# A normalised, quantised convolution on one core: another order of work for images 126 to 145, another beginning, and the last image's result in two places of PSUM

## The chip, the cores and the metric

The kernel runs on one core of a Trainium2 chip. The metric is the device time of one execution in microseconds (us). The engines are called as in the profile: PE (TensorE, the matrix engine; PEld is its loading of weights), DVE (VectorE), ACT (ScalarE), POOL (GpSimd), and SP, which here only issues DMAs. PSUM is the memory that PE writes its results to; all else is held in SBUF.

## The reference

`x` is 160 images of 128 channels of 32 x 32, in fp32. There are five sets of weights, and each belongs to 32 images. Cut to what matters:

```python
beta, alpha = max(U), min(U)                 # over all five sets
s1 = (beta - alpha) / 3.0
v1 = s1 * floor(U / s1)
s2 = s1 / 5.0
v2 = s2 * floor((U - v1) / s2)
w = v1 + v2                                  # 3x3, 128 -> 128 channels, per set
# group norm of each image, 32 groups of 4 channels, eps 1e-5
act = conv(gn(x), w, stride 1, padding 1)    # image of set n by the weights of set n
out = x + act
```

So no weight is known before all five sets (590 KB each) have been read for their extremes.

## The kernel before, in words

**Weights at the beginning.** `run` (L782) issues the loads of the five weight sets on SP's queue; sets 0 and 1 come in two transfers each (L793 to L795), and the first image's load lies behind set 2 (L797 to L799). DVE reduces each piece to its maximum and minimum (`weight_range`, L422; L429 and L430). `over_partitions` (L437) brings the extremes to all partitions, over two transposes on PE; between these and the rest it calls a function that it is given, here PE's part of the means of the first two images (L827). DVE then does a chain of small steps (`from_range`, L50): s1, its reciprocal and parts, s2 and its own. A column of the 3 x 3 weights of set 0 is quantised in steps of 384 elements per partition on DVE (`quantise`, L116, `floor_div`, L104), turned by PE (L472, into PSUM tile pt) and kept by ACT and POOL (`keep_column`, L478, into tile wt). The columns come in the order 1, 0, 2 (`COLS`). `run` is an order written out by hand: `take` and `run` place single steps of the chain and the columns between the steps of the images, and every engine works in the order in which its instructions are written. `warm_up` (L644) is a row of matmuls whose result is not used.

**Images.** There are two kinds. For a *plain* image, ACT normalises it (z, L523) and rounds it to half precision (hi, L531); DVE takes the rest (lo, L589) and combinations of lo's rows (rows, L603 to L606). For a *combined* image, POOL and DVE make combinations of rows of x itself (L554, L555; `combine`, L565 to L571), ACT scales and rounds these (vh, L576) and DVE takes the rest (vl, L582). From image 7 on every second image is combined, from image 146 on two of three (`combined`, L534).

**One pass.** From image 3 on, pass i of the loop at L902 has PE compute first the sums and differences of row pairs of image i+1 (`sums_of_pairs`, L681, into two PSUM tiles called m, `self.pair`; the second one, a = 1, first), then the rest of image i (`rest_of_column`, L708, into its PSUM tile eo). PE takes few instructions for a combined image and more for a plain one. Beside that

- DVE does vl (or lo and rows) of image i+2, now and then the residual of image i-1, `pairs` of image i+1, and `combine` of image i+4;
- ACT does the first statistics pass (L194), the half of the result of image i-1 (sum, L754), the copy of one of m's tiles (L725), vh (or z and hi) of image i+3, and the second statistics pass (L201);
- POOL does outer rows, small steps of the statistics, and issues the DMA that adds sum to x (L773).

`pairs(i)` (L728) is two DVE instructions, L735 and L737, which add and subtract the two halves of m into a fresh eo tile, on which PE then accumulates the rest. eo tiles come from a pool of two (L376), the m tiles from a pool of one.

**Residual and store.** `residual(i)` (L746) is done by ACT and POOL, or "by hand" on DVE (L765): for images 31 on with i % 8 == 7, and for the last four, which are stored one by one from L769. The last image is computed in halves of 16 rows (L699), its residual and stores too (L757). All other stores are issued in `store` (L775) for two images at once.

**Weights later on.** The next sets are quantised on DVE in single steps between the images (`later`, L940; `take(later, ...)` at L967, L1005 and L1009). While the first images of a set are worked on, these steps lie between the two instructions of `pairs` and elsewhere.

Of the kernel before, what the change touches and what calls it, by code (L numbers as in the profile page):

```python
# [33 lines left out]
class Steps:  # L34
# [15 lines left out]
    def from_range(self, extg):  # L50


        nc, col = self.nc, self.col

        def divide_exact(tag, q1, a, m):

            q0, rem = col(tag + "q0"), col(tag + "rem")
            yield nc.vector.tensor_scalar_mul(q0, a, 1.0 / m)
            yield nc.vector.scalar_tensor_tensor(rem, q0, -(m - 1.0), a, ALU.mult, ALU.add)
            yield nc.vector.tensor_sub(rem, rem, q0)  # L60
            yield nc.vector.scalar_tensor_tensor(q1, rem, 1.0 / m, q0, ALU.mult, ALU.add)

        def parts(out, s):

            r, neg, hi, lo = out
            yield nc.vector.tensor_scalar_mul(neg, s, -1.0)
            yield nc.vector.reciprocal(r, s)
            yield nc.vector.tensor_single_scalar(
                hi.bitcast(I32), neg.bitcast(I32), -4096, op=ALU.bitwise_and
            )  # L70
            yield nc.vector.tensor_sub(lo, neg, hi)

        span = col("span")
        yield nc.vector.tensor_reduce(span, extg, AX.X, ALU.add)
        yield from divide_exact("s1", self.s1, span, 3.0)

        of_s1, s2 = parts(self.parts1, self.s1), divide_exact("s2", self.s2, self.s1, 5.0)
        for chain in (s2, of_s1, of_s1, s2, of_s1, s2, s2, of_s1):
            yield next(chain)
        yield nc.vector.tensor_scalar_mul(self.lift, self.s2, LIFT)  # L80
        yield from parts(self.parts2, self.s2)
        self.span, self.big = span, col("big")
        yield nc.vector.tensor_reduce(self.big, extg, AX.X, ALU.max)
# [228 lines left out]
class Main:  # L312
# [25 lines left out]
    LOAD_LEAD = 18  # L338
    STEADY = 7
    BY_VECTOR = (8, 10, 11, 14, 19, 24, 29, 34)  # L340
    THIRDS = 146
    EARLY = 8
    FIRST = 3
# [78 lines left out]
    def weight_range(self, us):  # L422

        nc, P = self.nc, self.P
        halved = [part for u in us[:2] for part in (u[:, : P // 2], u[:, P // 2 :])]
        pieces = [*halved, *us[2:]]
        ext = self.const.tile([P, 2, len(pieces)], F32, tag="ext", name="ext")
        for k, piece in enumerate(pieces):
            nc.vector.tensor_reduce(ext[:, 0, k : k + 1], piece, AX.XY, ALU.max)  # L429
            nc.vector.tensor_reduce(  # L430
                ext[:, 1, k : k + 1], piece, AX.XY, ALU.min, negate=True
            )
        ext1 = self.const.tile([P, 2], F32, tag="ext1", name="ext1")
        nc.vector.tensor_reduce(ext1, ext, AX.X, ALU.max)
        return ext1

    def over_partitions(self, ext1, ident, between):  # L437


        nc, P = self.nc, self.P  # L440
        rows = self.ps_tr.tile([1, 2, P], F32, tag="pt", name="rows")
        for k in range(2):
            nc.tensor.transpose(rows[:, k, :], ext1[:, k : k + 1], ident)
        between()
        top = self.const.tile([1, 2], F32, tag="top", name="top")
        nc.vector.tensor_reduce(top, rows, AX.X, ALU.max)
        spread = self.ps_tr.tile([P, 2], F32, tag="pt", name="spread")
        nc.tensor.matmul(spread, self.ones, top, start=True, stop=True)
        return spread
# [44 lines left out]
    def by_vector(self, i):  # L494
        return i in self.BY_VECTOR

    def stats_of(self, k):
        if k not in self.stats:
            self.stats[k] = Statistics(
                self.nc, self.small, self.ps_stat, self.gavg, self.mhalf, len(self.groups[k]),  # L500
                self.steps.lift, k,
            )
        return self.stats[k]

    def measure(self, i, stages=(0, 1)):


        k = self.group_of[i]
        g = self.groups[k]
        st, j, image = self.stats_of(k), i - g.start, self.image(i)  # L510
        if self.by_vector(i):
            st.image(j, image)
            return
        for s in stages:
            junk = self.unread.tile([self.P, 1024], MM, tag="junk", name=f"junk{i}_{s}")
            (st.image_sum, st.image_square)[s](j, image, junk)

    def normalise(self, i):
# [7 lines left out]
        )  # L526
        self.z[i] = z

    def high_part(self, i):
        hi = self.parts.tile([self.P, self.H, self.W], MM, tag="hi", name=f"hi{i}")  # L530
        self.nc.scalar.copy(hi.rearrange("p h w -> p (h w)"), self.z[i])  # L531
        self.hi[i] = hi

    def combined(self, i):  # L534

        if i < self.STEADY or i >= self.imgs:
            return False

        return i % 2 == 1 if i < self.THIRDS else i % 3 != 1

    def column_of(self, i):

# [96 lines left out]
        return self.ps_eo.tile([self.P, 2, self.H // 2, self.W], F32, tag="eo", name=f"eo{i}")  # L639

    def bank(self, target, h):
        return target[h] if target is self.pair else target[:, h]

    def warm_up(self, count):  # L644

# [47 lines left out]
    def conv(self, i, on_the_way):  # L693


        if self.FIRST < i < self.imgs - 1:
            self.sums_of_pairs(i + 1)

        for halves in ((0,), (1,)) if i == self.imgs - 1 else ((0, 1),):  # L699
            for col in self.COLS:  # L700
                if col == self.COLS[2] and i == self.FIRST:
                    self.sums_of_pairs(i + 1)
                if col != self.COLS[0] and halves[-1] == 1:
                    on_the_way(col)
                self.rest_of_column(i, col, halves)
        del self.v[i]

    def rest_of_column(self, i, col, halves):  # L708
        eo, both = self.eo[i], self.both(i)
        if not self.combined(i):  # L710
            self.taps(i, (self.hi[i], 0), col, eo, False, halves)
        for a, kind in enumerate((0, self.MINUS_G2)):
            for j, (d, _) in enumerate(both):
                for h in halves:
                    rows = slice(h * 16 + a, h * 16 + 16, 2)
                    to = eo[:, h].rearrange("p (i a) w -> p a i w", a=2)[:, a]
                    self.product(
                        to, i, kind, d[:, rows, :], col, False,
                        col == self.COLS[-1] and a == 1 and j == len(both) - 1,
                    )  # L720
# [7 lines left out]
    def pairs(self, i, between=lambda: None):  # L728


        nc = self.nc
        m1, m2 = self.pair[0], self.m2.pop(i)
        eo = self.eo[i] = self.bank_pair(i)
        rows = eo.rearrange("p h (i a) w -> p (h i) a w", a=2)
        nc.vector.tensor_add(rows[:, :, 0], m1, m2)  # L735
        between()
        nc.vector.tensor_sub(rows[:, :, 1], m1, m2)  # L737
# [44 lines left out]
    def run(self):  # L782
# [4 lines left out]
        for n in range(N_SETS):  # L787
            if n == 0:
                un = self.upool.tile([P, P, TAPS], F32, tag="u", name="u0")
            else:  # L790
                un = self.space(f"range{n}").rearrange("p j e -> p (j e)")[:, : P * TAPS]
                un = un.rearrange("p (i k) -> p i k", k=TAPS)
            half = P // 2 if n < 2 else P  # L793
            for c in range(0, P, half):
                nc.sync.dma_start(un[:, c : c + half], self.uv[n][:, c : c + half])  # L795
            self.us[n] = un
            if n == 2:  # L797
                self.chunks[0] = self.space("xt0")
                nc.sync.dma_start(self.chunks[0][:, 0, :], self.xv[0, :, 0, :])  # L799
        nc.sync.dma_start(self.chunks[0][:, 1, :], self.xv[0, :, 1, :])  # L800
        for c in range(1, 6):
            self.load(c, single=c < 2)
        warm = self.const.tile([P, 1], F32, tag="warm", name="warm")
        nc.vector.memset(warm, 0.0)
# [16 lines left out]

        self.ones = self.const.tile([1, P], F32, tag="ones", name="ones")
        nc.vector.memset(self.ones, 1.0)
        ext1 = self.weight_range(list(self.us.values()))
        for i in range(2):
            self.measure(i)
        spread = self.over_partitions(ext1, ident, self.stats_of(0).means)  # L827

        def take(steps, count):
            for _ in range(count):  # L830
# [13 lines left out]
        first, second, third = (  # L844
            self.make_column(0, col, by_scalar=col != self.COLS[0]) for col in self.COLS
        )
        for ahead in (11, 2, 1, 1, 1, 1, 1, 1):
            take(chain, ahead)
            take(first, 1)
        run(chain)  # L850
        self.stats[0].deviations()
        measure(0, 2, 3)
        self.stats[0].variances()
        self.stats[0].deviation()
        measure(1, 2)
        self.stats[0].scales()
        take(second, 1)
        measure(1, 3)
        self.stats[1].means()
        self.stats[1].deviations()  # L860
        self.warm_up(14)
        parts(0)
        self.stats[1].variances()
        self.warm_up(8)
        self.stats[1].deviation()
        self.stats[1].scales()
        parts(1)
        run(first)
        self.warm_up(2)
        parts(2)  # L870
        take(second, 2)
        self.low_part(0)
# [29 lines left out]
        for i in range(self.imgs):  # L902
# [58 lines left out]
            else:  # L961
# [3 lines left out]
                elif i + 2 < self.imgs:  # L965
                    self.low_part(i + 2)
                    take(later, 1)  # L967
                    run(self.combinations(i + 2))
                if i > self.FIRST and self.by_hand(j):
                    self.residual(j)  # L970
                for k in by_scalar:
                    self.measure(k, (0,))
# [10 lines left out]
                for st in ready:  # L983
                    st.deviations()
                if part:
                    self.normalise(i + 3)
                    self.high_part(i + 3)
                if self.combined(i + 3):
                    self.high_combined(i + 3)
# [12 lines left out]
            if i >= self.FIRST:  # L1002
# [3 lines left out]
                if self.combined(i + 4):  # L1006
                    self.combine(i + 4)
                else:
                    take(later, 1)  # L1009
                if b == self.per_set - 4:  # L1010
                    run(later)
# [61 lines left out]
```

## Time and profile before

| | |
|---|---|
| median of 5 runs | 991.95 us |
| lowest, highest | 991.81, 992.79 us |
| profiled execution | 992.12 us |
| its span, from first to last instruction | 990.40 us |
| mean granted PE clock | 0.998 |
| mean DMA rate | 248 GB/s |
| read from, written to HBM | 89.19, 83.89 MB |

The profiled execution is longer than its span by 1.72 us. Some of the costliest groups (columns: line, engine, operation, output and inputs with their shapes, count; then busy us in all and mean ns of one):

```
L582 DVE SCALAR_TENSOR_TENSOR vl<-v,rstd,vh 128x2048 f16<-128x2048 f32 x80 | 188.2, 2352 | 4.1 <-ACT vh L576 4.1
L576 ACT ACTIVATE vh<-v,rstd 128x2048 f16<-128x2048 f32 x80 | 160.8, 2010 | 2.5 <-POOL v L555 2.0
L523 ACT ACTIVATE z<-xt,shift,rstd 128x1024 f32<-128x1024 f32 x80 | 99.8, 1248 | 2.6 <-POOL shift L244 2.6
L589 DVE TENSOR_TENSOR lo<-z,hi 128x1024 f16<-128x1024 f32 x80 | 97.9, 1224 | 0.0
```

How to read it: the last part of a line is the idle time of the engine just ahead of such instructions, and what ended most of it. The mean of a group hides no idle time, but an instruction may start later than the one before it ended; durations "from start to start" count that gap. In a row of windows, each engine's busy time in the stretch is followed by its number of instructions. In a row of single instructions, the first number is the start in us from the span's start, the second the busy time, and what stands in brackets is the idle time ahead of it and its releaser.

### The profile page before, as it was taken

To read this page: it belongs to the slowest core of one execution; us is meant where nothing else is said; L and a number is where in the kernel's file an instruction comes from. 1 tells how busy PE (TensorE), PEld (TensorE's weight loads), DVE (VectorE), ACT (ScalarE), POOL (GpSimd) and SP (SyncE) were. 2 spreads that over 40 slices of the span, in tenths; PEclk is the share of its full clock that TensorE was granted. 3 is DMA by queue.
4 is the path that set the end of the run, shared out by engine and by line. 5 is a ranking of instruction groups with operands and counts; after the bars stand their busy time and mean duration, and the time that the engine had idled before them with its cause. 6 is when DMAs were issued, how large, how long until landed. Compare 5 with 4: busy or idle time off the path is not lost.

```text
span 990.4 us, 16124 instructions
## 1 busy us (share of the span) xinstructions
PE 959.7 (97%) x5938; PEld 578.8 (58%) x5938; DVE 928.5 (94%) x1256; ACT 895.6 (90%) x1224; POOL 387.5 (39%) x565
## 2 busy tenths in 40 slices
PE   2999999999999999999999999999999999999997
PEld 1445655566656666666665666666665666666564
DVE  7999999999999999999999999999999998889995
ACT  5879999999999999999999999999999999998651
POOL 4425563644316253414263443315343424132410
PEclk9999999999999999999999999999999999999999
DMA  9538999999997999898989999997999898987764
GB/s 357 211 103 238 237 255 274 257 265 270 260 303 181 298 249 294 237 282 244 273 218 266 274 279 236 281 282 223 237 280 304 214 300 217 293 227 206 180 178 153
DMA packets 65129, 246.05 MB, mean 248 GB/s; under 512 B 5008, under 2 KB 5008, under 8 KB 65040
## 3 DMA queue, kind: packets, MB, share of 16 engines
q1 hardware_dynamic: 45312, 173.09, 49.9%
q0 software_dynamic: 19728, 71.84, 37.7%
q8 instruction: 48, 0.79, 0.3%
q14 instruction: 41, 0.34, 0.1%
HBM read 89.19 MB, written 83.89 MB: 175 GB/s over the span
## 4 chain that ended last, share of the span: by engine, by line
PE 74%; DVE 12%; ACT 7%; issue 3%; POOL 2%; DMA 0%; SPq 0%; DVEq 0%; ACTq 0%; POOLq 0%
PE eo L668 24%; PE m L668 24%; PE eo L629 24%; ACT vh L576 2%; ACT junk L201 2%; ACT sum L754 1%; DVE eo L737 1%; DVE eo L735 1%; DVE lo L589 1%; DVE v L565 1%; POOL v L554 1%; DVE vl L582 1%; ACT m L725 1%; DVE v L568 1%; DVE v L571 1%
## 5 line engine op out<-in xcount | busy, mean ns | idle before, releaser
L668 PEld LDWEIGHTS <-wt 128*128 128x128 f16 x4266 | 417.2, 98 | 235.3 <-issue 7.2
L629 PE MATMUL eo<-hi,wt 128*128 128x496 f16 (+3 forms) x1422 | 340.8, 376 | 1.4 <-ACT wt L485 0.9
L773 POOL DMA_DIRECT2D xt<-sum x137 | 122.9, 903 | 460.2 <-ACT sum L754 445.5
L629 PEld LDWEIGHTS <-wt 128*128 128x128 f16 x1494 | 146.5, 99 | 142.5 <-issue 2.2
L582 DVE SCALAR_TENSOR_TENSOR vl<-v,rstd,vh 128x2048 f16<-128x2048 f32 x80 | 188.2, 2352 | 4.1 <-ACT vh L576 4.1
L668 PE MATMUL m<-vh,wt 128*128 128x496 f16 (+1 forms) x480 | 182.2, 380 | 2.0 <-DVE eo L737 1.2
L668 PE MATMUL eo<-vh,wt 128*128 128x248 f16 (+1 forms) x960 | 184.0, 273 | 0.0
L668 PE MATMUL eo<-vl,wt 128*128 128x248 f16 (+1 forms) x960 | 183.9, 273 | 0.0
L668 PE MATMUL m<-vl,wt 128*128 128x496 f16 (+1 forms) x480 | 182.2, 380 | 0.2 <-DVE vl L582 0.2
L194 ACT ACTIVATE junk<-xt 128x1024 f16<-128x1024 f32 x152 | 160.6, 1057 | 15.8 <-DMA xt<-in_x_dram 12.3
L201 ACT ACTIVATE junk<-xt,mv 128x1024 f16<-128x1024 f32 x152 | 173.8, 1144 | 0.1
L576 ACT ACTIVATE vh<-v,rstd 128x2048 f16<-128x2048 f32 x80 | 160.8, 2010 | 2.5 <-POOL v L555 2.0
L754 ACT ACTIVATE sum<-eo 128x1024 f32<-128x1024 f32 x137 | 138.2, 1008 | 15.3 <-PE eo L668 15.2
L735 DVE TENSOR_TENSOR eo<-m,m 128x512 f32<-128x512 f32 x157 | 109.1, 695 | 35.3 <-ACT m L725 28.2
L668 PE MATMUL eo<-rows,wt 128*128 128x256 f16 (+1 forms) x924 | 138.9, 273 | 0.0
L668 PE MATMUL m<-rows,wt 128*128 128x496 f16 (+1 forms) x462 | 113.6, 380 | 0.4
L737 DVE TENSOR_TENSOR eo<-m,m 128x512 f32<-128x512 f32 x157 | 109.4, 697 | 3.6
L725 ACT COPY m<-m 128x512 f32<-128x512 f32 x157 | 90.7, 577 | 18.4 <-PE m L668 18.4
L523 ACT ACTIVATE z<-xt,shift,rstd 128x1024 f32<-128x1024 f32 x80 | 99.8, 1248 | 2.6 <-POOL shift L244 2.6
L589 DVE TENSOR_TENSOR lo<-z,hi 128x1024 f16<-128x1024 f32 x80 | 97.9, 1224 | 0.0
L565 DVE TENSOR_TENSOR v<-xt 128x960 f32<-128x960 f32 x80 | 91.9, 1148 | 0.0
L531 ACT CAST hi<-z 128x1024 f16<-128x1024 f32 x80 | 83.6, 1045 | 2.5
(111 smaller groups left out, 892.4 us busy)
## 6 DMA issues: line engine op xcount, KB each, us to landing
xt<-in_x_dram SPq DMA_DIRECT2D x78, 1024.0 KB, 9.5
out_dram<-xt SPq DMA_DIRECT2D x78, 1024.0 KB, 5.9
xt<-sum POOLq DMA_DIRECT2D x137, 512.0 KB, 6.1
u<-in_L_conv_U_dram SPq DMA_DIRECT2D x4, 576.0 KB, 9.5
xt<-in_x_dram SPq DMA_DIRECT2D x4, 512.0 KB, 9.6
range<-in_L_conv_U_dram SPq DMA_DIRECT2D x3, 576.0 KB, 8.0
out_dram<-xt SPq DMA_DIRECT2D x3, 512.0 KB, 2.9
u<-in_L_conv_U_dram SPq DMA_DIRECT2D x2, 288.0 KB, 3.0
```

The lines of the kernel that those rows point to most:

```text
L194: self.nc.scalar.activation(junk, image, ACTF.Copy, scale=-1.0 / image.shape[1], accum_out=self.mv[:, j, 0:1],)
L201: self.nc.scalar.activation(junk, image, ACTF.Square, bias=self.mv[:, j, 0:1], accum_out=self.mv[:, j, 1:2],)
L565: nc.vector.tensor_sub(v[:, W:last], x[:, : last - W], x[:, 2 * W :])
L576: self.nc.scalar.mul(vh, self.v[i], st.rstd[:, j])
L582: self.nc.vector.scalar_tensor_tensor(vl, self.v[i], st.rstd[:, j], self.hi[i], ALU.mult, ALU.subtract)
L589: self.nc.vector.tensor_sub(lo[:, 1 : self.H + 1, :].rearrange("p h w -> p (h w)"), self.z.pop(i), self.hi[i].rearrange("p h w -> p (h w)"),)
L629: nc.tensor.matmul(self.bank(target, h)[:, r0 - h0 : r1 - h0, c0:c1], self.wts[n, col][:, k, :], tile[:, s0 : s0 + r1 - r0, c0 + dw : c1 + ...
L668: self.nc.tensor.matmul(target[:, :, c0:c1], self.wts[n, col][:, kind, :], source[:, :, c0 + dw : c1 + dw], start=start, stop=stop, skip_g ...
L735: nc.vector.tensor_add(rows[:, :, 0], m1, m2)
L737: nc.vector.tensor_sub(rows[:, :, 1], m1, m2)
L754: nc.scalar.mul(self.sum[i], eo.rearrange("p h r w -> p (h r w)"), 0.5)
L773: self.nc.gpsimd.dma_start(self.image(i), self.sum.pop(i), accum_op=ALU.add)
```

## The change

It has three parts.

1. **Images 126 to 145.** Combined are now the first, third and fifth of each five images (126, 128, 130, 131, 133, 135, ...), 12 of the 20 where it was 10. The fourth of each five (129, 134, 139; not 144, the first image of its statistics group) is plain, but its z is computed on DVE, by one tensor-scalar instruction at the end of pass i-4, where `combine` lies for combined images. ACT still makes its hi.
2. **The beginning.** Weight set 1 comes in one transfer. The first image's loads lie behind all five sets. The chain of small steps is s1, all parts of s1, s2, and so on, with no interleaving, and the steps of the first column are taken at other places of it. The statistics of images 0 and 1 are written behind the chain; PE's part of their means is no longer between the transposes and the rest. `warm_up` is called with 14 and 7 and no longer with 14, 8 and 2; the order of the parts of image 1 changes around it.
3. **The last image.** Its eo is two PSUM tiles, one per half of 16 rows, each with its own `pairs`. Those of the second half are made between PE's work on the two halves, behind the residual of image 158, since the eo pool still has two tiles.

The diff's core:

```diff
-        of_s1, s2 = parts(self.parts1, self.s1), divide_exact("s2", self.s2, self.s1, 5.0)
-        for chain in (s2, of_s1, of_s1, s2, of_s1, s2, s2, of_s1):
-            yield next(chain)
+        yield from parts(self.parts1, self.s1)
+        yield from divide_exact("s2", self.s2, self.s1, 5.0)
...
+    FIFTHS = 126
     THIRDS = 146
...
-        halved = [part for u in us[:2] for part in (u[:, : P // 2], u[:, P // 2 :])]
-        pieces = [*halved, *us[2:]]
+        pieces = [us[0][:, : P // 2], us[0][:, P // 2 :], *us[1:]]
...
+    def normalise_by_vector(self, i):
+        st, j = self.column_of(i)
+        z = self.z[i] = self.zpool.tile([self.P, 1024], F32, tag="z", name=f"z{i}")
+        self.nc.vector.tensor_scalar(
+            z, self.image(i), st.rstd[:, j], st.shift[:, j], ALU.mult, ALU.add
+        )
...
-        return i % 2 == 1 if i < self.THIRDS else i % 3 != 1
+        if i < self.FIFTHS:
+            return i % 2 == 1
+        return (i - self.FIFTHS) % 5 % 2 == 0 if i < self.THIRDS else i % 3 != 1
+
+    def by_vector_too(self, i):
+
+        if not self.FIFTHS <= i < self.THIRDS or (i - self.FIFTHS) % 5 != 3:
+            return False
+
+        return i != self.groups[self.group_of[i]].start
...
         for halves in ((0,), (1,)) if i == self.imgs - 1 else ((0, 1),):
+            if halves == (1,):
+                self.residual(i - 1)
+                self.pairs(i)
...
-        m1, m2 = self.pair[0], self.m2.pop(i)
-        eo = self.eo[i] = self.bank_pair(i)
-        rows = eo.rearrange("p h (i a) w -> p (h i) a w", a=2)
+        m1, m2 = self.pair[0], self.m2[i]
+        if i == self.imgs - 1:
+
+            h = len(self.eo.setdefault(i, []))
+            eo = self.bank_pair(f"{i}_{h}")[:, 0]
+            self.eo[i].append(eo)
+            part = slice(h * self.H // 4, (h + 1) * self.H // 4)
+            m1, m2 = m1[:, part], m2[:, part]
+        else:
+            eo = self.eo[i] = self.bank_pair(i)
+            eo = eo.rearrange("p h r w -> p (h r) w")
+        rows = eo.rearrange("p (i a) w -> p i a w", a=2)
...
-            half = P // 2 if n < 2 else P
+            half = P // 2 if n == 0 else P
...
-            if n == 2:
-                self.chunks[0] = self.space("xt0")
-                nc.sync.dma_start(self.chunks[0][:, 0, :], self.xv[0, :, 0, :])
-        nc.sync.dma_start(self.chunks[0][:, 1, :], self.xv[0, :, 1, :])
-        for c in range(1, 6):
+        for c in range(6):
             self.load(c, single=c < 2)
...
-        ext1 = self.weight_range(list(self.us.values()))
-        for i in range(2):
-            self.measure(i)
-        spread = self.over_partitions(ext1, ident, self.stats_of(0).means)
+        spread = self.over_partitions(self.weight_range(list(self.us.values())), ident)
...
-        for ahead in (11, 2, 1, 1, 1, 1, 1, 1):
+        for ahead in (8, 1, 1, 1, 1, 1, 3, 1, 1, 1):
             take(chain, ahead)
             take(first, 1)
         run(chain)
+        measure(0, 0, 1)
+        measure(1, 0, 1)
+        self.stats[0].means()
         self.stats[0].deviations()
         measure(0, 2, 3)
         self.stats[0].variances()
         self.stats[0].deviation()
+        take(second, 1)
         measure(1, 2)
         self.stats[0].scales()
-        take(second, 1)
         measure(1, 3)
         self.stats[1].means()
         self.stats[1].deviations()
         self.warm_up(14)
         parts(0)
         self.stats[1].variances()
-        self.warm_up(8)
         self.stats[1].deviation()
         self.stats[1].scales()
-        parts(1)
+        self.normalise(1)
         run(first)
-        self.warm_up(2)
+        self.warm_up(7)
+        self.high_part(1)
...
-                    self.normalise(i + 3)
+                    if not self.by_vector_too(i + 3):
+                        self.normalise(i + 3)
                     self.high_part(i + 3)
...
                 if self.combined(i + 4):
                     self.combine(i + 4)
                 else:
+                    if self.by_vector_too(i + 4):
+                        self.normalise_by_vector(i + 4)
                     take(later, 1)
```

More of the change, by code (lines that the diff above doesn't have):

```diff
@@ L435, in weight_range, with over_partitions @@
         return ext1
-    def over_partitions(self, ext1, ident, between):
+    def over_partitions(self, ext1, ident):
         nc, P = self.nc, self.P
@@ L443, in over_partitions @@
             nc.tensor.transpose(rows[:, k, :], ext1[:, k : k + 1], ident)
-        between()
         top = self.const.tile([1, 2], F32, tag="top", name="top")
@@ L495, in by_vector @@
         return i in self.BY_VECTOR
[L497 to L503, printed above, removed]
     def measure(self, i, stages=(0, 1)):
@@ L509, in measure @@
         g = self.groups[k]
-        st, j, image = self.stats_of(k), i - g.start, self.image(i)
+        if k not in self.stats:
+            self.stats[k] = Statistics(
+                self.nc, self.small, self.ps_stat, self.gavg, self.mhalf, len(g),
+                self.steps.lift, k,
+            )
+        st, j, image = self.stats[k], i - g.start, self.image(i)
         if self.by_vector(i):
@@ L527, in normalise @@
         self.z[i] = z
+    def normalise_by_vector(self, i):
[3 more added lines that the diff above has]
+            z, self.image(i), st.rstd[:, j], st.shift[:, j], ALU.mult, ALU.add
+        )
     def high_part(self, i):
@@ L641, in bank @@
     def bank(self, target, h):
-        return target[h] if target is self.pair else target[:, h]
+        return target[h] if isinstance(target, list) else target[:, h]
     def warm_up(self, count):
@@ L715, in rest_of_column @@
                     rows = slice(h * 16 + a, h * 16 + 16, 2)
-                    to = eo[:, h].rearrange("p (i a) w -> p a i w", a=2)[:, a]
+                    to = self.bank(eo, h).rearrange("p (i a) w -> p a i w", a=2)[:, a]
                     self.product(
@@ L968, in run @@
                     run(self.combinations(i + 2))
-                if i > self.FIRST and self.by_hand(j):
+                if i > self.FIRST and self.by_hand(j) and j in self.eo:
                     self.residual(j)
```

## The prediction

> **What bounds it.** I read the page's busy shares and clock row, then the windows of single stretches, the waits, and the order in time at three places.
>
> ```profile
> PE 959.7 (97%) x5938; PEld 578.8 (58%) x5938; DVE 928.5 (94%) x1256; ACT 895.6 (90%) x1224; POOL 387.5 (39%) x565
> ...
> PE 74%; DVE 12%; ACT 7%; issue 3%; POOL 2%; DMA 0%; SPq 0%; DVEq 0%; ACTq 0%; POOLq 0%
> ```
>
> PE bounds nearly everything, but DVE and ACT have 3 to 7% to spare, so what relieves PE must be weighed against both. Windows (columns: stretch, its us, PE, PEld, DVE, ACT, POOL busy, granted clock, DMA share, GB/s), of one plain and one combined image, and of two combined and one plain:
>
> ```profile
> 798.35:809.99 11.64, 11.64 (x74) 7.05 (x72) 10.06 (x14) 11.54 (x16) 1.45 (x3) 1.00 0.93 267
> ...
> 928.07:944.93 16.86, 16.86 (x111) 10.57 (x109) 16.61 (x19) 9.68 (x10) 3.93 (x8) 1.00 0.77 202
> ```
>
> PE is gapless in both. 16.86 − 11.64 = **5.22 us for a combined image**, 11.64 − 5.22 = **6.42 us for a plain one**: 1.20 us apart. From the order in time, a combined image is 2.59 (m) + 2.63 (eo), a plain one 1.30 + 5.12.
>
> **Part 1: images 126 to 145.** Combined images go from 10 to 12 of 20: PE −2 × 1.20 = **−2.40 us**. ACT: a combined image costs 1.90 from start to start (L576), a plain one 1.28 + 0.95 (L523, L531); common work is 3.70. Three combined, two plain, one z given away: 3 × 5.60 + 2 × 5.93 − 1.28 = 27.4 of PE's 3 × 5.22 + 2 × 6.42 = 28.5 in five images. DVE from start to start: combine 2.33, vl 2.26, lo with its rows 2.53, pairs 1.34, a by-hand residual 1.35. Five images: 3 × 5.93 + 2 × 3.87 + z 0.75 + 5/8 × 1.35 = 27.1 of 28.5. So it fits on average; the order decides.
>
> Pass i gives PE m(i+1), then eo(i): 7.71 if i is plain and i+1 combined, 3.93 the other way, 5.22 for two combined. DVE gets vl or lo of i+2, perhaps a residual, pairs(i+1), then combine or z of i+4. PE's second half of m(i+1) overwrites what pairs(i) reads, so a late pairs stops PE. The trace has one such place, just past three combined images:
>
> ```profile
> 917.42 0.70 DVE L735 TENSOR_TENSOR eo<-m,m 128x512 f32<-128x512 f32 x1
> ...
> 918.15 0.70 DVE L737 TENSOR_TENSOR eo<-m,m 128x512 f32<-128x512 f32 x1
> ...
> 918.42 0.38 PE L668 MATMUL m<-vl,wt 128*128 128x496 f16 x1
> ...
> 918.90 0.38 PE L668 MATMUL m<-vh,wt 128*128 128x512 f16 x1
> ```
>
> PE could have gone on at 918.64; it goes on at 918.90, as the second pairs instruction ends (918.85). I carried these durations through the new order by hand, each start being the latest of its engine's and its inputs' times. Done for the old order from 773.46 on, the end of the last matmul comes out at 983.93; the trace has 983.79. In the new order four places stop PE:
> - Pass 124. DVE used to end pass 122 at 773.77; combine(126) is now there: 773.24 + 2.33 = 775.57, vl(125) to 777.83, pairs(124) with a weight step in between to 779.79. PE would start that half at 778.83: **1.0 us**.
> - Pass 129. The residual of 127 used to lie in a pass of 7.71; pass 128 now has 3.93. DVE runs without a gap from pairs(127) at 794.77 (released by ACT's copy): 1.34 + 2.33 + 2.53 + 1.34 + 2.33 + 2.26 + 1.35 + 1.34 + 0.09 = 14.9, to 809.7. PE from 795.59: 2.59 + 5.12 + 1.30 + 2.63 + 1.30 = 12.9, to 808.5: **1.2 us**.
> - Passes 132 and 134: **0.4 and 0.5 us**, the same kind, after two combined images in a row.
> The other by-hand residual in a short pass (136) comes out without a gap, as DVE is less behind there. The stops sum to 3.1; the bookkeeping is 0.2 too hard on the old order, so I take 2.9: −2.4 + 2.9 = **+0.5 us**. Ends: all stops covered, −2.4; z at one element a cycle (no row has it: lo<-z,hi of the same size takes 1.22), +1.1.
> Z in between: nn<-rest, a tensor-scalar of 384 elements, takes 0.41, tt<-tt,s2r,nn, with two tensors, 0.61; the 0.2 less is 384 at half a cycle of about 1.04 ns, so I put z at 0.41 + 640 × 0.52 ns = 0.75. The Trainium skill's VectorE: DVE Perf Modes, Mode 2×_2P, says that a single-source fp32 instruction in SBUF gets two elements a cycle; at one a cycle the sum would be 0.4 higher.
>
> POOL's outer rows move with the combined images and have 60% free. No DMA is added; SP's stores move with PE.
>
> **Part 2: the beginning goes back.** The second weight set comes in one transfer, x0 behind all sets.
>
> ```profile
> 6.65 0.75 DVE L429 TENSOR_REDUCE ext<-range 128x1 f32<-128x576 f32 x1 [0.34 <-DMA range<-in_L_conv_U_dram]
> ...
> 9.30 1.34 DVE L429 TENSOR_REDUCE ext<-range 128x1 f32<-128x1152 f32 x1
> ...
> 39.06 0.46 PE L472 MATMUL pt<-ident,k 128*128 128x128 f16 x5 [1.38 <-DVE k L114]
> ...
> 40.10 2.69 PE L629 MATMUL eo<-hi,wt 128*128 128x496 f16 x6 [0.58 <-ACT wt L485]
> ```
>
> Two whole-set reductions take 2.52, four halves took 2.65, so DVE is even if set 1 lands at 6.78. The second half landed 5.1 after its issue at 2.14, at 7.24; with one issue less I take 7.1: DVE **+0.32**. In the chain of small steps s1r comes sooner and three small steps more lie among the big ones: 28.19 becomes 28.09, **−0.10**. Images 0 and 1 land at about 12.9 and 14.2 (10.1 and 14.3), so ACT and POOL run later: z(0) at 25.8 (23.59), hi(1) done at 32.15 (29.37), hi(2) at 34.4. DVE's lo(1) waits 0.2 more. Weight column 0 is ready 0.4 late and PE starts it at 40.6 (40.10). What hides that is PE's own pause, with the clock behind it:
>
> ```profile
> 38.00:39.00 1.00, 0.00 (x0) 0.00 (x0) 0.90 (x3) 0.00 (x0) 0.00 (x0) 1.00 0.00 0
> 39.00:40.00 1.00, 0.46 (x5) 0.29 (x5) 0.96 (x3) 0.44 (x2) 0.00 (x0) 0.98 0.00 0
> 40.00:41.00 1.00, 0.90 (x3) 0.34 (x4) 0.93 (x2) 1.00 (x3) 0.49 (x1) 0.50 0.00 0
> ...
> 43.00:44.00 1.00, 1.00 (x5) 0.44 (x4) 0.94 (x2) 1.00 (x2) 0.59 (x1) 0.81 0.00 0
> ```
>
> PE is idle from 37.7 to 39.06 and 39.5 to 40.10, and from 40.0 to 43.4 the clock is half: the first 12 matmuls take 4.15 us (40.10 to 44.25) and not 2.55, 1.6 lost. Starting later on the images, PE is now busy until about 39.5 and pauses 0.6, so I expect the clock to stay: five blocks of 1.28 from 40.6 end at 47.0 (48.06 before). Column 2 then waits for ACT, whose unbroken row of 9.0 us from wt to wt puts it at 49.65 (49.80). **−0.1 us**, and +0.5 if the clock falls again.
> The Trainium skill's TensorE: Matmul & The Clock Gate, What's actually happening, says the clock halves after an idle window of about 3.4 us. The half-rate stretch is indeed 3.4, but here 1.4 + 0.6 us of pause with work between were enough, so I trust the row; by the page neither version falls, the old start gains 1.6 that the trace denies it, and my sum is unchanged.
>
> **Part 3: the last image.**
>
> ```profile
> 981.37 1.23 DVE L765 SCALAR_TENSOR_TENSOR xt<-eo,xt 128x1024 f32<-128x1024 f32 x1 [1.14 <-PE eo L668]
> 984.00 1.29 DVE L765 SCALAR_TENSOR_TENSOR xt<-eo,xt 128x512 f32<-128x512 f32 x2 [1.40 <-PE eo L668]
> ```
>
> Now one residual half may start as soon as its own matmuls end. But eo has two buffers: half 1 goes where image 158 lies, so its pairs waits for residual(158), queued ahead of it on DVE, and PE waits for pairs. Residual 981.37 + 1.35, two 256-column instructions (0.46 + 0.43, from 0.73 and 0.70 for 512 less 256 cycles), 0.06 to PE: half 1 starts at 983.67, not 982.48. Its 12 matmuls of 0.109 and 0.32 of pipeline give 985.19, its residual of 0.68 ends at 985.87, not 985.29: +0.58. The first half's store leaves 0.5 sooner, out of the last one's way (3.1 us to land, 2.7 the quickest): **+0.45**, ends 0 and +0.6.
>
> **Sum.** −0.1 + 0.5 + 0.45 = +0.85. The profiled execution took 992.12 (span 990.40 + 1.72), 0.17 above the median of the runs shown. 990.40 + 0.85 + 1.72 = 992.97, less 0.17: **992.8 us**, no change to speak of (0.2%, 2.0 us, is what a measurement of this kernel can tell).
>
> **Rivals.**
> - Faster, 989.9 (10%): DVE keeps up. −0.1 − 2.4 + 0.45 = −2.05. For it: DVE's average fits. Against: the stop at 918.90. It sits on the 0.2% line.
> - Slower, 994.5 (12%): set 1, now one transfer, shares the DMA engines with set 2 and lands with it, at about 8.8 (issued 2.56, 6.2 to land). The reductions then start 1.7 later than forecast, and each us past 7.1 costs one, as the cover of PE's pause is used up: 992.8 + 1.7. From a landing at about 8.3 on, it is slower by over 0.2%. Against: the two halves, issued 0.43 apart, landed 0.6 apart, one after the other.
> - The clock falls at 40 again, 993.4 (10%).
> - The tail does what it says, 991.7 (8%): the stores gain 0.6, not −0.45.
> - Forecast 992.8 (60%), alone 991.8 to 993.8.
> Faster by over 0.2%: half of the first, 5%. Slower: the second and a little of the third, 14%. Within: 81%. The range 990.8 to 994.4 leaves out the outer parts of the first two.
>
> **What will show it.** PE gaps of about 1 us at the passes of images 124 and 129, each ending with a pairs instruction; z below 0.9 us; a granted clock of 1.0 from 40 to 43; the first whole-set reduction near 7.1; an idle PE of 1.2 us between the last image's halves. Gaps missing from the first two would prove part 1 wrong by up to 2.9; a first reduction past 8 would prove part 2 wrong.

## The result, and the profile after

The changed kernel is **slower by 0.16%**: the ratio of its runs to those of the kernel before is 1.0016 (95% interval 1.0011 to 1.0022; 25 runs beside 45; it is that of the means, and the medians, 994.41 and 992.31 us, would give 1.0021). On the 991.95 us shown at first that is 993.5 us. The forecast was 992.8 within 990.8 to 994.4, "no change to speak of" within 0.2%. The sign holds and the time lies in the range, but the +0.85 of the forecast lies below the 1.1 to 2.2 that were measured; as the traces show, two of its three terms are near the forecast's and the third is not.

The page of the profiled execution (994.89 us, span 993.1), its busy shares and the shares of the chain that ended last:

```profile
PE 956.6 (96%) x5935; PEld 578.1 (58%) x5935; DVE 933.8 (94%) x1259; ACT 891.7 (90%) x1219; POOL 397.9 (40%) x569
...
PE 67%; DVE 15%; ACT 8%; issue 4%; POOL 3%; DMA 3%; SPq 0%; DVEq 0%; POOLq 0%; ACTq 0%
```

PE is busy 3.1 us less and the span is 2.7 us longer: PE has less to do, as was meant, and stops have more than eaten that. To see where, I compared the start of the second `pairs` instruction of each image in the two traces. After less before it is +1.44 us at image 6 and still +1.45 at image 114; +1.38 at image 123; it moves between +0.75 and +4.6 from 124 to 139; and it is +1.98 from image 146 to 158. The span ends 2.7 later. So the **beginning cost 1.44, images 126 to 145 0.55, the last image 0.7**.

*The beginning.* DVE's reductions in order of time (start, busy time, engine and line), first the last one of the kernel before, then the changed kernel's:

```profile
16.98 0.17 DVE L434 TENSOR_REDUCE ext<-ext 128x2 f32<-128x14 f32 x1
```

```profile
8.10 1.35 DVE L427 TENSOR_REDUCE ext<-range 128x1 f32<-128x1152 f32 x1 [1.60 <-DMA range<-in_L_conv_U_dram]
...
18.31 0.17 DVE L432 TENSOR_REDUCE ext<-ext 128x2 f32<-128x12 f32 x1
```

Set 1 is there at 8.1, not at 7.1; DVE stands for 1.60 us, and the last reduction comes 1.33 us later than in the kernel before (16.98). Next, the columns, three engines put together, again the kernel before first:

```profile
39.56 0.49 ACT L485 ACTIVATE wt<-pt 128x384 f16<-128x384 f32 x1 [3.13 <-PE pt L472]
48.59 0.49 ACT L485 ACTIVATE wt<-pt 128x384 f16<-128x384 f32 x1
52.46 0.39 PE L227 MATMUL pg<-dv,gavg 128*128 128x4 f32 x2
```

```profile
41.16 0.49 ACT L481 ACTIVATE wt<-pt 128x384 f16<-128x384 f32 x1 [1.58 <-PE pt L468]
41.70 1.44 PE L638 MATMUL eo<-hi,wt 128*128 128x496 f16 x6 [0.58 <-ACT wt L481]
50.05 0.47 ACT L481 ACTIVATE wt<-pt 128x384 f16<-128x384 f32 x1
50.58 1.45 PE L638 MATMUL m<-hi,wt 128*128 128x496 f16 x6 [0.61 <-ACT wt L481]
53.65 0.20 POOL L222 TENSOR_TENSOR dv<-dv,mv 128x4 f32<-128x4 f32 x1
53.90 0.39 PE L225 MATMUL pg<-dv,gavg 128*128 128x4 f32 x2 [0.61 <-POOL dv L222]
```

The copy of column 0 is 1.60 later than before (39.56), ACT's row from the copy of column 0 to that of column 2 is 8.89 (before: 9.03), and behind the copy of column 2 POOL makes the weights' combinations and then the statistics that PE's next matmul waits for: 53.90, where it was 52.46. The windows show that PE's clock holds (busy us and instructions of PE, PEld, DVE, ACT, POOL, granted clock, DMA share, GB/s):

```profile
41.00:42.00 1.00, 0.42 (x5) 0.18 (x3) 0.93 (x3) 0.84 (x3) 0.00 (x0) 1.00 0.00 0
42.00:43.00 1.00, 1.00 (x7) 0.44 (x6) 0.97 (x2) 1.00 (x3) 0.81 (x2) 1.00 0.08 16
```

*Images 126 to 145.* The waits of PE between 770 and 860 (us in total, times, longest; the kernel before has none there), and DVE's row in front of the longest:

```profile
PE m L677 <- DVE eo L758: 1.6, 2, 1.1
```

```profile
803.60 1.15 DVE L574 TENSOR_TENSOR v<-xt 128x960 f32<-128x960 f32 x1
...
805.93 2.35 DVE L591 SCALAR_TENSOR_TENSOR vl<-v,rstd,vh 128x2048 f16<-128x2048 f32 x1
808.19 1.22 DVE L786 SCALAR_TENSOR_TENSOR xt<-eo,xt 128x1024 f32<-128x1024 f32 x1
809.54 0.70 DVE L756 TENSOR_TENSOR eo<-m,m 128x512 f32<-128x512 f32 x1
810.28 0.70 DVE L758 TENSOR_TENSOR eo<-m,m 128x512 f32<-128x512 f32 x1
...
811.03 0.38 PE L677 MATMUL m<-vh,wt 128*128 128x512 f16 x1 [1.12 <-DVE eo L758]
```

This is the row of pass 129: combine, vl, the by-hand residual of image 127 (L786), and then `pairs`, without a gap from one to the next. PE, which is ready at 809.75, starts at 811.03. Z by DVE (line, then shortest, median and longest in ns):

```profile
L525 DVE TENSOR_SCALAR z<-xt,rstd,shift x3: 804/804/805, 792.8 to 851.3; 128x1024 f32<-128x1024 f32 x3
```

*The last image*, DVE and PE together:

```profile
983.35 1.23 DVE L786 SCALAR_TENSOR_TENSOR xt<-eo,xt 128x1024 f32<-128x1024 f32 x1 [1.67 <-PE eo L677]
984.61 0.43 DVE L756 TENSOR_TENSOR eo<-m,m 128x256 f32<-128x256 f32 x1
985.08 0.43 DVE L758 TENSOR_TENSOR eo<-m,m 128x256 f32<-128x256 f32 x1
985.42 0.68 DVE L786 SCALAR_TENSOR_TENSOR xt<-eo,xt 128x512 f32<-128x512 f32 x1
985.57 0.28 PE L677 MATMUL eo<-vh,wt 128*128 128x256 f16 x1 [0.94 <-DVE eo L758]
987.09 0.69 DVE L786 SCALAR_TENSOR_TENSOR xt<-eo,xt 128x512 f32<-128x512 f32 x1 [0.99 <-PE eo L677]
```

PE stands between the halves, for image 158's residual and the second half's pairs ahead of it on DVE. The last residual ends at 987.78, which is 2.49 later than before, 0.5 of it beyond the 1.98 that image 158 already carries.

### The profile page after: what moved, and what is told of

Read it like the earlier page. It is cut to its first block, busy times and chain, and to the rows that moved or that the text cites. A ratio compares the mean times of both kernels' runs of the same rounds, so it can differ in the third digit from the quotient of the medians.

```text
span 993.1 us, 16119 instructions
## 1 busy us (share of the span) xinstructions
PE 956.6 (96%) x5935; PEld 578.1 (58%) x5935; DVE 933.8 (94%) x1259; ACT 891.7 (90%) x1219; POOL 397.9 (40%) x569
## 4 chain that ended last, share of the span: by engine, by line
PE 67%; DVE 15%; ACT 8%; issue 4%; POOL 3%; DMA 3%; SPq 0%; DVEq 0%; POOLq 0%; ACTq 0%
PE eo L677 22%; PE m L677 22%; PE eo L638 21%; DVE eo L756 2%; DVE eo L758 2%; ACT junk L199 2%; ACT vh L585 2%; DVE v L574 2%; DVE vl L591 2%; DVE lo L598 1%; DMA xt<-sum 1%; ACT sum L775 1%; POOL v L563 1%; DVE v L577 1%; DVE v L580 1%
## 5 line engine op out<-in xcount | busy, mean ns | idle before, releaser
L638 PE MATMUL eo<-hi,wt 128*128 128x496 f16 (+3 forms) x1386 | 331.0, 375 | 1.1 <-ACT wt L481 0.6
L591 DVE SCALAR_TENSOR_TENSOR vl<-v,rstd,vh 128x2048 f16<-128x2048 f32 x82 | 193.0, 2354 | 2.0 <-ACT vh L585 2.0
L677 PE MATMUL m<-vh,wt 128*128 128x496 f16 (+1 forms) x492 | 186.7, 380 | 3.5 <-DVE eo L758 2.7
L677 PE MATMUL eo<-vh,wt 128*128 128x248 f16 (+1 forms) x984 | 188.6, 273 | 0.9 <-DVE eo L758 0.9
L677 PE MATMUL eo<-vl,wt 128*128 128x248 f16 (+1 forms) x984 | 188.5, 273 | 0.0
L677 PE MATMUL m<-vl,wt 128*128 128x496 f16 (+1 forms) x492 | 186.7, 380 | 0.3 <-DVE vl L591 0.2
L585 ACT ACTIVATE vh<-v,rstd 128x2048 f16<-128x2048 f32 x82 | 164.8, 2010 | 3.6 <-POOL v L564 1.9
L756 DVE TENSOR_TENSOR eo<-m,m 128x512 f32<-128x512 f32 (+1 forms) x158 | 109.4, 692 | 32.8 <-ACT m L737 21.9
L758 DVE TENSOR_TENSOR eo<-m,m 128x512 f32<-128x512 f32 (+1 forms) x158 | 109.7, 694 | 3.7
L516 ACT ACTIVATE z<-xt,shift,rstd 128x1024 f32<-128x1024 f32 x75 | 93.6, 1248 | 2.6 <-POOL shift L242 2.6
L563 POOL TENSOR_SCALAR v<-xt,ngm 128x32 f32<-128x32 f32 x82 | 84.5, 1031 | 0.1
```

The costliest lines, as they stand in the source:

```text
L585: self.nc.scalar.mul(vh, self.v[i], st.rstd[:, j])
L591: self.nc.vector.scalar_tensor_tensor(vl, self.v[i], st.rstd[:, j], self.hi[i], ALU.mult, ALU.subtract)
L638: nc.tensor.matmul(self.bank(target, h)[:, r0 - h0 : r1 - h0, c0:c1], self.wts[n, col][:, k, :], tile[:, s0 : s0 + r1 - r0, c0 + dw : c1 + ...
L677: self.nc.tensor.matmul(target[:, :, c0:c1], self.wts[n, col][:, kind, :], source[:, :, c0 + dw : c1 + dw], start=start, stop=stop, skip_g ...
```

## The experiments

Theory 1 is the reading above: the landing of set 1 sets the beginning, and DVE's late pairs set the rest. Theory 2, which came later, adds that the loads of images must not come late either. The rivals stand with each run. "From 118 to 158" and the like mean by how much the lag behind the trace of the kernel before grows or shrinks between those images.

**The three parts alone.** Each was put into the kernel before by itself: the new beginning, `FIFTHS` with `normalise_by_vector`, and the last image's two tiles.

> The kernel before with the new beginning alone. Theory 1 (set 1's landing): in the trace of after the first reduction of set 1 starts at 8.10 us, the chain is 1.33 late, and the lateness goes through the copy of weight column 0 on ACT into ACT's row of 8.9 us up to the copy of column 2; PE is 1.44 late from then on. So +1.4 us, the same from image 3 to the last, if set 1 lands at 8.1. Rival (as forecast): PE's pause of 2 us covers it, -0.1 to +0.2 us. A landing of 7.1 instead would show in the first reduction and give about +0.3 by theory 1 as well; the runs of after lay between 992.6 and 995.3 us, so I expect the landing to differ from run to run.

> The kernel before with only the other order of images 126 to 145. Theory 1: +0.5 us; PE gains 2.4 and loses 3.0 in six stops, each ended by a pairs instruction on DVE: 0.9 in pass 124, 1.3 in pass 129, 0.4 in pass 132, 0.5 in pass 134. Rival: those stops belong to the late start, not to the order; then the part alone shows fewer of them and is faster, down to -2.4 us.

> The kernel before with only the last image's halves in two places. Theory 1: +0.5 to +0.7 us; PE stops for about 1.1 us between the halves, until DVE has done the residual of image 158 and the second half's pairs, and the last residual ends 0.5 later than before. Rival: the first half's store leaves 0.6 sooner and the last store gains from it: -0.6 to 0 us.

Measured: 1.0011 (1.0002 to 1.0020), 1.0007 (0.9998 to 1.0016) and 1.0000 (0.9991 to 1.0009). They add up to 1.0018, near the 1.0016 of the whole. The traces say more than these ratios, whose intervals are about as wide as the effects. The new beginning alone:

```profile
8.87 1.35 DVE L427 TENSOR_REDUCE ext<-range 128x1 f32<-128x1152 f32 x1 [2.53 <-DMA range<-in_L_conv_U_dram]
```

and its window up to there:

```profile
0.00:8.80 8.80, 0.00 (x0) 0.00 (x0) 2.94 (x6) 1.47 (x2) 6.59 (x16) 1.00 0.74 257
```

Here set 1 is there at 8.87, and image 60 is 1.70 late. The rival (PE's pause covers it) falls. By 8.80 us the DMA engines had moved 8.80 x 257 GB/s = 2.26 MB, 3.8 sets of 590 KB, though set 1 is the second in the queue. In the changed kernel it was 8.00 x 233 = 1.86 MB, 3.2 sets:

```profile
0.00:8.00 8.00, 0.00 (x0) 0.00 (x0) 2.94 (x6) 1.47 (x2) 6.61 (x16) 1.00 0.70 233
```

So the sets behind it are under way while set 1 is not complete. They still land in the order of the queue, set 2 1.4 us after set 1 in both traces (9.52 and 10.30). The images alone have the same stops as the changed kernel, to 0.01 us: 0.22 and 0.66 in pass 124, 1.28 in pass 129, 0.36 in pass 132, 0.49 in pass 134, together 3.0 (counted from start to start of PE's matmuls); they belong to the order and not to the late start. From 118 to 158 they cost 0.6. The tail alone has the stop of 1.10, and its last residual ends 0.50 late again, as measured from image 158. The rival of e2 falls; for the tail, the ratio excludes only a loss of more than 0.9 us.

**Set 1 in two transfers again**, all else as in the changed kernel (the reductions go by halves again too):

```diff
...
-            half = P // 2 if n == 0 else P
+            half = P // 2 if n < 2 else P
```

> The changed kernel with one thing undone: weight set 1 comes in two transfers again and is reduced in halves. Theory 1 (the landing sets the beginning): the first half lands near 6.6 us, the reductions end 1.1 to 1.3 sooner and the kernel is 1.1 to 1.3 us faster than the changed one: about +1.2 us against the kernel before, not +2.7. Rival (the order of the statistics and of the first image's loads sets it): no difference from the changed kernel.

Measured: 1.0002 (0.9993 to 1.0011), and image 60 is 0.36 *ahead* of the kernel before, 1.8 ahead of the changed one. The 0.36 is within what the old beginning does by itself: in the nine other traces that have it unaltered, image 60 lies between 0.01 behind and 0.67 ahead. The first half is there before DVE is done with set 0:

```profile
5.62 0.75 DVE L429 TENSOR_REDUCE ext<-u 128x1 f32<-128x576 f32 x1
6.28 0.75 DVE L428 TENSOR_REDUCE ext<-range 128x1 f32<-128x576 f32 x1
```

The new order of the chain and the statistics costs next to nothing: from the last reduction to the copy of column 0 it takes 22.70 us here and 22.58 in the kernel before. One transfer in place of two is the beginning's whole price, somewhat more than the theory said. And it is not only that a first half can be used early: in two transfers the whole of set 1 was there at 7.05 (the second half was issued at 2.18 and took 4.9), in one at 8.1 and 8.9.

**Another order of the images: 130 to 144, no by-hand residual.** Two more combined images as in the change, four residuals fewer on DVE.

```diff
+    FIFTHS, FIFTHS_END = 130, 145
...
-        return i > self.BY_VECTOR[-1] - 4 and i % 8 == 7
+        return i > self.BY_VECTOR[-1] - 4 and i % 8 == 7 and i < 127
```

> The kernel before with 130 to 144 in fives instead of 126 to 145 (again two combined images more than before; z by DVE for 133, 138 and 143), and the residuals of 127, 135, 143 and 151 done by ACT and POOL and no longer by hand on DVE. Theory 1 (DVE's late pairs cost the gain): combine no longer lies in the passes with weight steps, no by-hand residual lies in a short pass; the same bookkeeping of instructions that gave the stops of the changed order gives none here: -2.4 us, no stop over 0.2 between 770 and 860. Rival (DVE and ACT are too full for 12 combined images of 20 in any order, ACT now with four sums more): stops of 1 us and more remain, -1 to +0.5 us.

Measured: 1.0026 (1.0017 to 1.0035). **The theory's number failed**, by about 5 us in the ratio and by 4.3 in the trace from 123 to 158. The waits of ACT and of PE between 770 and 925:

```profile
ACT junk L194 <- DMA xt<-in_x_dram: 6.7, 5, 2.7
```

```profile
PE m L685 <- ACT m L742: 1.0, 2, 0.6
PE m L685 <- DVE vl L599: 0.8, 1, 0.8
PE m L685 <- DVE rows L623: 0.7, 1, 0.7
PE m L685 <- DVE eo L754: 0.5, 1, 0.5
```

Pass 124 and pass 129 have no stop, as expected. But ACT now waits 6.7 us for images that have not been loaded, which the bookkeeping of instructions knows nothing of, and PE stops at 847 to 860 and, about twice as long in all, from 906 to 920, behind 144 to 147, four combined images in a row where the kernel before has three: the end of my own pattern. So I took the two edits apart.

> The kernel before with one thing changed: the residuals of 127, 135, 143 and 151 are done by ACT and POOL's adding DMA instead of by hand on DVE. Theory 2 (the four adding DMAs make the loads of images late): ACT waits for images for several us between 770 and 925 (none in the kernel before), and stops of PE ended by ACT's copy show up at 846 and 906: +0.5 to +2 us. Rival (in the run with 130 to 144 in fives the order of images itself made the loads late): no wait of ACT for images, 0 us.

Measured: 1.0003 (0.9994 to 1.0013), no stop of PE that the kernel before does not have. ACT's waits for images, 770 to 925 (the kernel before has none there):

```profile
ACT junk L194 <- DMA xt<-in_x_dram: 2.0, 2, 1.4
```

**Theory 2 falls in this form**, and so does the rival's "no wait of ACT": the four adding DMAs alone make ACT wait for 2.0 us and raise the DMA share from 0.88 to 1.01 between 860 and 890, but stop PE nowhere. With them and the faster order the loads are late; how much of e6's loss is theirs and how much the four combined images' stays open. Outside the traces there is a little more: the executions of e6, e8 and e11, the three that take the residuals off DVE, last 2.0, 2.1 and 1.9 us longer than their spans (medians), those of all others 1.7 to 1.8.

> The kernel before with images 130 to 139 alone in fives (one combined image more than before, z by DVE for 133 and 138) and the by-hand residuals as before. Those of 127, 135 and 143 then lie in long passes, no combine lies beside weight steps, and the loads of images are relieved as before. Theory 2 (the gain of an extra combined image, 1.20 us, is there as long as neither DVE's order nor the loads of images stop PE): -1.2 us, no stop over 0.2 between 770 and 860, ACT waits for no image between 770 and 925. Rival (an extra combined image costs elsewhere what it gives PE, whatever the order): 0.

(`FIFTHS_END = 140`, the residuals untouched.) Measured: **0.9985** (0.9976 to 0.9994). From 123 to 158 the lag shrinks by 1.23, and 1.20 was the price of one image. ACT does wait for an image, which was not expected, once and for 1.3 us, but no stop of PE follows from it. The only wait of PE between 770 and 925 is one that the kernel before has too:

```profile
PE m L685 <- DVE vl L599: 0.2, 1, 0.2
```

> The kernel before with images 130 to 144 in fives whose first, second and fourth are combined (two combined images more than before), z by DVE for the third of each five (132, 137, 142), by-hand residuals as before. By the bookkeeping of instructions DVE stops PE for 0.9 in all: -1.5 us by theory 2. Rival (two more combined images in 15 are more than DVE's order or the loads bear): stops of 2.4 us and more, 0 to +1.

(`in (0, 1, 3)` in place of `% 2 == 0`.) Measured: **0.9982** (0.9973 to 0.9991). From 126 to 158 the lag shrinks by 1.54, with three stops of about 0.25 (0.9 was expected in all): two more combined images pay if they are laid where DVE has the time.

**The last half in the second m tile**, which is free as soon as ACT has copied it:

```diff
+        if i == self.imgs - 1:
+            self.eo[i] = [self.bank_pair(i)[:, 0], self.pair[1]]
...
```

> The kernel before with the last image's second half in the second m tile, which is free once ACT has copied it, so that neither half waits for image 158; both halves' pairs lie where the one pair lay. Theory 1 (the second half's wait for the eo buffer cost the tail): no stop of PE between the halves, the first half's residual ends near 983.5 and the last at 984.7 where it was 985.3: -0.4 to -0.6 us. Rival: the last store's landing is bound by the stores ahead of it, so 0.

Measured: 0.9998 (0.9989 to 1.0007). DVE's row at the end:

```profile
980.99 2.00 DVE L773 SCALAR_TENSOR_TENSOR xt<-eo,xt 128x1024 f32<-128x1024 f32 x2 [0.87 <-PE eo L668]
983.62 0.69 DVE L773 SCALAR_TENSOR_TENSOR xt<-m,xt 128x512 f32<-128x512 f32 x1 [0.62 <-PE m L668]
```

and the last line of the DMA view from 979 us on (queue, count, KB each, median us from issue to landing), first of the kernel before, then of this one:

```profile
out_dram<-xt SPq DMA_DIRECT2D x2, 256.0 KB, 3.1
```

```profile
out_dram<-xt SPq DMA_DIRECT2D x2, 256.0 KB, 4.3
```

The stop is gone and the last residual ends at 984.31; taken from image 158 it is 0.60 sooner than in the kernel before. But the two last stores take 4.3 us to land, 3.1 before, and from the last residual to the end of the span it is 5.99, not 5.11. The rival holds in its outcome: what DVE gains, the stores give back, in this trace more than that. Whether the stores ahead of the last one delay it, as the rival has it, was not tested.

> Both edits together (130 to 144 in fives, residuals 127 to 151 off DVE, last half in the second m tile). Theory 1: the gains add, -2.8 to -3.0 us, 0.3% faster than the kernel before. Rival: as for the two alone, -1 to +0.5 us.

> Images 130 to 139 in fives, by-hand residuals as before, and the last image's second half in the second m tile. Theory 2: the two gains add, -1.2 and -0.4 to -0.6: about -1.7 us. Rival: 0.

Measured: 1.0020 (1.0012 to 1.0029) for the first, which has e6's stops, and **0.9983** (0.9974 to 0.9992) for the second: 0.3 us shorter than e10's in the traces (988.3 beside 988.6), with the last residual 0.59 sooner; the stores gave half of it back. e10, e12 and e13 are faster than the kernel before; between the three no difference is shown.

**The clock kept up**, by matmuls of zeros in PE's pauses:

```diff
+        self.keep_warm(6)
         measure(0, 4, 5)
         take(third, 1)
         measure(1, 4)
         run(second)
+        self.keep_warm(3)
```

> The kernel before with nine matmuls of zeros, accumulated onto image 2's tile, six in PE's pause at 37.7 to 39.0 and three in that at 39.5 to 40.1. Theory 1 (column 2 waits for ACT's row whatever PE does): the granted clock stays at 1.0 from 40 to 44, PE is ready 0.6 to 1.4 sooner and waits for the copy of column 2 instead; 0 to -0.3 us. Rival: the 1.6 us lost at half the clock come back, -1.2 to -1.6 us.

Measured: 1.0000 (0.9992 to 1.0009). The window at 41, and PE's row at column 2:

```profile
41.00:42.00 1.00, 1.00 (x7) 0.44 (x5) 0.90 (x2) 1.00 (x3) 0.92 (x3) 1.00 0.00 0
```

```profile
48.91 1.45 PE L629 MATMUL m<-hi,wt 128*128 128x496 f16 x6 [0.60 <-ACT wt L485]
...
52.23 0.39 PE L227 MATMUL pg<-dv,gavg 128*128 128x4 f32 x2 [0.61 <-POOL dv L224]
```

The clock stays at 1.00; PE is ready sooner and waits twice for 0.6 us. The 1.6 us lost at half the clock were worth nothing.

## Why the prediction was right or wrong

- **Part 1, +0.5: right, by its own steps.** The four places are there with their sizes: 0.9 in pass 124 (1.0 forecast), 1.3 in pass 129 (1.2), 0.4 and 0.5 in passes 132 and 134 (0.4 and 0.5), together 3.0 (2.9). The long ones are ended by a pairs instruction, as forecast; two of 0.23, in passes 124 and 134, are ended by vl, also on DVE. Against 2.4 saved it makes 0.55 in the changed kernel, 0.6 alone. Z took 0.80 where 0.75 was put; the other end, one element a cycle, is out. e10 and e13 show the other side: with no such place the gain is 1.2 for one image, and with 0.8 of stops it is 1.5 for two.
- **Part 2, −0.1: wrong by 1.5, as its own sign ("a first reduction past 8") says, and two steps failed.** The first is *"with one issue less I take 7.1"* for the landing of set 1: it landed at 8.1 and 8.9. I had carried over the time at which a second half landed (7.34 in the trace; I had read 7.24) to a whole set in one transfer. In two transfers the whole set was there at 6.1 to 7.5 in all twelve traces that have it so, so it is the single transfer that is late; why, stays open. The slower rival, 8.8, has the time about right, but not its mechanism: set 2 does not land with set 1. The second is that PE's start on column 2 would be the end of the matter. PE did start it only 0.78 late, as its own delay by the clock fell away; but its next matmul waits for POOL, whose work follows the copy of column 2 by a fixed row: 3.87 us before, 3.85 after, 3.85 in e9. The chain is: the last reduction, 22.5 to 22.9 to column 0's copy, 8.9 to 9.1 to column 2's, 3.85 to PE; PE's pause is not in it, and its clock hardly. By that chain the forecast's own column 0, 0.5 late, would have cost 0.4 to 0.5; the 1.33 of the reductions cost 1.44, and in e1, where they were 2.09 late, 1.8 at image 6.
- **The clock**: expected to hold, and it held. But that it held says little: of the ten traces with the old order of the beginning and nothing added in PE's pauses, it fell in three (the kernel before, e2, e11), with first pauses of 1.2 to 1.9 us, and held in seven, with 1.1 to 1.9. So the fall varies between executions, and the prediction, which read the one trace as a rule, was wrong to. The Trainium skill's TensorE: Matmul & The Clock Gate, What's actually happening, calls the number of slow matmuls at a kernel's start variable from run to run, as the window of activity runs freely. Three falls in ten would fit such a window; no run here shows it.
- **Part 3, +0.45: right in its mechanism, short by 0.3 in the trace.** PE's stop is 1.1 (1.2 forecast), the last residual is 0.50 late (0.58). The stores did not give 0.13 back but cost 0.2 more: 0.7 in the trace. The measured ratio of the part alone, 1.0000 ± 0.0009, neither confirms nor excludes this.
- **The sum.** The parts in the traces are 1.44 + 0.55 + 0.7 = 2.7, the measured ratio says 1.1 to 2.2. The landing of set 1 may be the difference: it differed by 0.8 between the two traces that have it in one transfer, and the changed kernel's runs lie between 992.6 and 995.3. Where it lay in the other runs was not seen, so this stays open. That the time still fell into the range owes something to luck: with the 2.7 of the traces it would have been 994.6, above the 994.4 that the range ends at.

## What to carry to other kernels

Where the last engine has little to spare beside the first, an average that fits decides nothing: add up both in the order in which the instructions stand, pass by pass, and move the extra work to the long passes; the same gain per image was lost in the order from 126 on and was had in that from 130 to 139. But such a sum counts only what is in it: when an order gets faster, look also at the loads that must come sooner. And before a pause is counted as cover, follow the late result through every engine that starts its next row with it.

## What was not expected of the hardware

A 590 KB load that is the second in its queue was complete only after 3.2 and 3.8 times its size had been moved in all, all five sets being queued together; cut in two, its first half landed at 5.3 to 6.6 us and the whole at 6.1 to 7.5, in all twelve traces that have it so. The Trainium skill's DMA: Bandwidth & Descriptors, Queues, rings and completion order, says that each DMA engine takes the descriptors of a ring in order, and that completion is not first in, first out for an issuing engine; by order alone I would have expected about two sets to be moved by then, which is an estimate. The sets themselves did land in order (8.08, 9.52, 10.94 and 12.37 in the changed kernel). Which of the 16 engines was behind, the traces do not show.
